# Selective scan: the rate product moved into the banks of y, y copied out in two passes, sums of a block begun later

## The chip, the cores and the metric

The kernel runs on one core of a Trainium2 chip. The metric is the device time of one execution in microseconds (us). Four compute engines work side by side, each through its own list of instructions in order: TensorE (PE: matrix products and transposes), VectorE (DVE), ScalarE (ACT) and GpSimd (POOL). Transfers are issued by these engines or by SyncE (SP) and run on 16 DMA engines. An instruction waits where a semaphore that it names has not been reached, and everything behind it on its engine waits too. PE writes its results into PSUM, a small memory in banks; 128 partitions of 1024 float32 values take two banks.

## The reference

Layer 0 is an attention over pairs, layer 1 a block with a selective scan. Nearly the whole time goes into the four scans of layer 1, cut here to what matters:

```python
delta = softplus(dts + dt_bias)                  # the "rate", one per token and channel
def step(h, inp):
    d_t, x_t, B_t, C_t = inp
    dA = exp(d_t[..., None] * As)
    h = dA * h + (d_t * x_t)[..., None] * B_t[:, :, None, :]
    y = einsum('bkdn,bkn->bkd', h, C_t)          # sum over the 16 states
    return (h, y)
# four orders of the 256 x 256 tokens: by rows, by columns, and both backwards
y = out_y[:, 0] + inv_y[:, 0] + wh_y + invwh_y
```

There are 65,536 tokens, 256 channels (two halves of 128) and 16 states. `dts` is a product of an 8-row matrix with the scan's own weights; the bias is a ninth row.

## The kernel before

`build` runs group statistics, a layer norm, the attention, a convolution, a transposition of one scratch tensor, `scans`, and `output`. `scans` (line 620) goes through the four orders one after the other, each in 64 blocks of 1024 tokens (`TB`), 256 blocks in all. A block has 32 half steps: half step `s` is state `m = s // 2` and channel half `h = s % 2`. The blocks of a scan are written out in a loop body of 18 blocks, run three times, with 4 blocks ahead of it and 6 behind; the instructions are issued in the order written (`manual_schedule`).

The work of a half step `s`, in the order of `body` (line 926):

- `recur(s)` (DVE, line 875): one scan instruction over 128 x 1024 values. It reads the decay `da` and the input `d1` and writes `hs`. After the second half DVE reduces the last column into `state`, and POOL multiplies both halves of `hs` by `cc` (the C of the reference, line 882).
- `turn(s + 1)` (PE, lines 863 and 865): fills `d1` of the next half step, 3 of its 8 pieces by a product with diagonal matrices and 5 by transposing pieces of `but`. `d1` lies in one of only two PSUM tiles `mm` (ring of two, function `mm()`), handed out in turn.
- `collect_some` (PE, line 617 in `turned`): transposes multiplied pieces of `hs` from six half steps (`LAG * NH`) earlier and adds them up in the PSUM tiles of y. Eight pieces come in for each half step; the most that are taken is 10, or what the table `share` says for this half step. The tiles of y still hold the block before until its last pieces are in (half step 5), so the pieces of a new block wait until a tile is in the set `free`.
- `decay(s + 4)` and `scale(s + 4)` (ACT, lines 856 and 852): the exponential `da` (a ring of six) and two or three of the five pieces of `but`.

The pieces of the next block's preparation are spread over these half steps by the list at the end of `begin` (line 751). Each entry is (half step, whether at its end, function). `rate(h)` (PE, line 764) is the product of the nine rows with the weights; `size(h)` (ACT, lines 773 and 774) reads it twice, into `e` (absolute value) and `delta` (positive part); `exp`, `log`, `one_plus` and `rest` are four ACT passes over 128 x 2048 values; `add` is a transfer issued by POOL (line 792) that adds `e`, `lw` or `w` to `delta` in memory; `turn_rate(i)` (PE, line 799) transposes half of the finished `delta` into an `mm` tile, and `times_x(i)` (DVE, line 803) multiplies that into `dxt`, which the next block's `scale` and `turn` read. `spread(g)` is a small ACT copy and a transfer.

In the kernel before, `rate` takes an `mm` tile, so a block hands out 36 of them: 32 for `d1`, two for the rate, two for `turn_rate`. y is four PSUM tiles of 512 values (`pys`); `evict` (ACT, line 915) copies two of them at half step 6 and two at half step 8, and puts them into `free`.

Of the kernel before, what the change touches and what calls it, by code (L numbers as in the profile page):

```python
# [35 lines left out]
P = 128  # L36
# [4 lines left out]
DI = 256  # L41
# [578 lines left out]
def scans(tc, io, c):  # L620
# [11 lines left out]
    nc = tc.nc  # L632
    TB = 1024
    NJ = TB // P
# [4 lines left out]
    PB = T // DI  # L639
    with tc.tile_pool(name="e_w", bufs=1) as wp, tc.tile_pool(name="e_1", bufs=1) as sb1, tc.tile_pool(  # L640
# [11 lines left out]
        def ring(name, n, shape, pool=wp):  # L652
            return [pool.tile(shape, F32, name=f"{name}{i}") for i in range(n)]
# [21 lines left out]
        das = ring("da", DA, [P, TB])  # L675
        hss = ring("hs", HS, [P, NH, TB])
        mms = ring("mm", 2, [P, TB], psum)
        pys = ring("y", NJ // PB, [P, PB, DI], psum)
        count = [0]

        def mm():
            count[0] += 1
            return mms[count[0] % 2]
# [67 lines left out]
        def begin(B):  # L751


            k = B.S.k
            B.pu, B.e = {}, None

            def rate(h):
                if B.e is None:  # L760
                    B.e = sb1.tile([P, NH, TB], F32, name="e")
                pu = B.pu[h] = mm()
                for q in range(0, TB, T):
                    nc.tensor.matmul(  # L764
                        pu[:, q : q + T],
                        dtw[0 : DR + 1, k, h * P : (h + 1) * P],
                        B.dt[0 : DR + 1, q : q + T],
                        start=True,
                        stop=True,
                    )  # L770

            def size(h):
                nc.scalar.activation(B.e[:, h, :], B.pu[h], AF.Abs)  # L773
                nc.scalar.activation(B.delta[:, h, :], B.pu[h], AF.Relu)

            def exp():
                nc.scalar.activation(B.e, B.e, AF.Exp, scale=-1.0)

            def log():
                B.lw = sb1.tile([P, NH, TB], F32, name="lw")  # L780
                nc.scalar.activation(B.lw, B.e, AF.Ln, bias=1.0)

            def one_plus():
                B.w = sb1.tile([P, NH, TB], F32, name="w")
                nc.scalar.activation(B.w, B.e, AF.Identity, bias=1.0)

            def rest():

                nc.scalar.activation(B.w, B.w, AF.Identity, scale=-1.0, bias=1.0)

            def add(name):
                nc.gpsimd.dma_start(out=B.delta, in_=getattr(B, name), accum_op=ALU.add)

            def turn_rate(i):
                B.pt = mm().rearrange("p (j d) -> p j d", d=DI)
                for j in range(NJ // 2):
                    for h in range(NH):
                        at = (i * NJ // 2 + j) * P
                        nc.tensor.transpose(B.pt[:, j, h * P : (h + 1) * P], B.delta[:, h, at : at + P], c.ident)

            def times_x(i):
                G = N // P
                nc.vector.tensor_tensor(  # L803
                    B.dxt[:, i * NJ // 2 : (i + 1) * NJ // 2, :].rearrange("p (w g) c -> p w g c", g=G),
                    B.pt.rearrange("p (w g) c -> p w g c", g=G),
                    B.in_order(B.xk, i, 2),
                    ALU.mult,
                )

            def spread(g):  # L810
                z = zs[0]
                first, step = B.slot(by_diagonal[0]), B.slot(by_diagonal[1]) - B.slot(by_diagonal[0])
                nc.scalar.copy(  # L813
                    z[:, P - 1 : P - 1 + GS * DJ * P].rearrange("p (m j q) -> p j m q", j=DJ, q=P)[:, :, :, 0],
                    B.bt[:, first : first + step * (DJ - 1) + 1 : step, g * GS : (g + 1) * GS],
                )
                nc.scalar.dma_start(out=B.apart(g), in_=z)

            pieces = [(4 + 6 * g, True, spread, g) for g in range(DS // GS)]
            return sorted(pieces + [  # L820
                (1, False, rate, 0),
                (1, True, size, 0),
                (3, False, rate, 1),
                (3, True, size, 1),
                (4, True, exp),
                (5, True, add, "e"),
                (9, True, log),
                (12, True, one_plus),
                (12, True, add, "lw"),
                (14, True, rest),  # L830
                (18, True, add, "w"),
                (25, False, turn_rate, 0),
                (25, True, times_x, 0),
                (27, False, turn_rate, 1),
                (27, True, times_x, 1),
            ], key=lambda x: x[:2])
# [70 lines left out]
                    collect(*x)  # L907
                    most -= 1

        def evict(B, after, part):  # L910

            n = NJ // PB // 2
            for g in range(part * n, (part + 1) * n):
                to = B.y[:, g * PB : (g + 1) * PB, :]
                nc.scalar.copy(to, pys[g])  # L915
                if after:
                    after.free.add(g)

        def add_y(B):
            nc.gpsimd.dma_start(out=B.rows(io["y"]), in_=B.as_rows(B.y), accum_op=ALU.add)  # L920

        U = NH * DS

        share = {1: 7, 3: 7, 6: 0, 7: 8, 8: 0, 25: 5, 27: 5}

        def body(blocks, before, after):

            own = len(blocks)
            at_hand = dict(enumerate(blocks + after))
            if before:  # L930
                at_hand[-1] = before
                before.free = before.started = set(range(NJ // PB))
                d1s[:] = [mms[count[0] % 2]]

            def at(u):
                x, s = divmod(u, U)
                return (at_hand[x], *divmod(s, NH)) if x in at_hand else None

            def do(f, u):
                if at(u):  # L940
                    f(*at(u))

            if before is None:
                blocks[0].load()
                blocks[0].load_tokens(0)
                blocks[0].load_tokens(1)
                blocks[0].advance(U, True)
                blocks[0].free = set(range(NJ // PB))
                blocks[1].load()
                for m in range(4):  # L950
                    fetch(blocks[0], m)
                for m in range(DG - 1):
                    diagonal(blocks[0], m)
                for u in range(2 * NH):
                    do(scale, u)
                for u in range(4):
                    do(decay, u)
                do(turn, 0)
            for x, B in enumerate(blocks):
                nxt = at_hand.get(x + 1)  # L960
                for s in range(U):
                    u = x * U + s
                    m, h = divmod(s, NH)
                    if s in (0, 8) and nxt:
                        nxt.load_tokens(s // 8)
                    if s == 21 and x + 2 in at_hand:
                        at_hand[x + 2].load()
                    if nxt:
                        nxt.advance(s, False)
                    if h == 0 and at(u + (DG - 1) * NH):  # L970
                        diagonal(*at(u + (DG - 1) * NH)[:2])
                    recur(B, m, h)
                    do(turn, u + 1)
                    if at(u - LAG * NH):
                        waiting.extend((*at(u - LAG * NH), j) for j in range(NJ))
                    collect_some(len(waiting) if s == LAG * NH - 1 else share.get(s, 10))
                    if x - 1 in at_hand and s in (6, 8):
                        evict(at_hand[x - 1], B, (s - 6) // 2)
                    if x - 1 in at_hand and s == 22:
                        add_y(at_hand[x - 1])  # L980
                    if nxt:
                        nxt.advance(s, True)
                    do(decay, u + 4)
                    if u == 0:
                        nc.scalar.preload_act_table_set("natural_log_exp_and_others")
                    do(scale, u + 2 * NH)
                    if h == NH - 1 and at(u + 1 + 3 * NH):
                        fetch(*at(u + 1 + 3 * NH)[:2])
            if not after:
                waiting.extend((*at(u), j) for u in range(own * U - LAG * NH, own * U) for j in range(NJ))  # L990
                collect_some(len(waiting))
                for part in range(2):
                    evict(blocks[-1], None, part)
                add_y(blocks[-1])
            assert not waiting


        n = NT // TB
# [160 lines left out]
```

## Time and profile before

| what | us |
|---|---|
| median of 3 runs (28149.8 to 28175.03) | 28162.98 |
| the profiled execution | 28147.05 |
| its span | 28145.4 |
| of it ahead of the scans, 0 to 4700 | 4700 |
| the scans, 4700 to 27360 | 22660 |
| the output stage, 27360 to the end | 786 |
| PE busy over the span | 25532.2 (91%) |
| DVE busy | 23715.0 (84%) |
| ACT busy | 23406.4 (83%) |
| POOL busy | 21571.6 (77%) |

The busy shares are means over stages with different limits. A PE that counts as busy need not run at full speed: matmuls are pipelined, and the column PEclk gives the clock that was granted as a share of full speed (0.976 over this span). The waits behind an engine's idle time are inferred from semaphore events, and a wait for several is put down to the one that came last. In a timeline a line is: start in us, length in us, engine, line of the kernel, operation, output and input tile, shape, how many in a row, and in square brackets the idle time ahead of it with what ended it.

### The profile page before, as it was taken

Reading aid. Unit: us, or ns where it says so; the run is one execution under the profiler, and the core shown is the slowest. Engines: PE = TensorE matmul, PEld = TensorE weight load, DVE = VectorE, ACT = ScalarE, POOL = GpSimd, SP = SyncE. Lnnn points to the kernel's source line nnn. Section 1 sums busy time; section 2 is a strip of 40 time slices with the busy share of each in tenths; the row PEclk is TensorE's granted clock in tenths of the full one; section 3 lists DMA queues with packets and bytes.
Section 4 is the critical chain, followed back from the end, with each engine's and each line's share of the span. In section 5 each row is a group of like instructions: output and inputs, shape, how many; then the busy total and the mean of one; then the engine's idle time right before and its main releaser. Section 6 shows DMA issues by size and latency. Waiting matters only on the chain. (4 is left out here: it accounts for less than half of the span.)

```text
span 28145.4 us, 510228 instructions
## 1 busy us (share of the span) xinstructions
PE 25532.2 (91%) x186250; PEld 20995.3 (75%) x186250; DVE 23715.0 (84%) x22718; ACT 23406.4 (83%) x39945; POOL 21571.6 (77%) x10118
## 2 busy tenths in 40 slices
PE   8999996999999999999999999999999999999988
PEld 3555443888888888888888888888888888888874
DVE  4777665888888888888888888888888888888887
ACT  6886223998989989989899899898998998989987
POOL 2443001998989989989899888888888888888883
PEclk9999997999999999999999999999999999999999
DMA  5112436888888888888888777777777777777775
GB/s 209 51 55 67 114 110 143 233 233 230 233 230 233 233 229 232 233 228 233 227 234 234 226 232 233 230 233 230 232 233 231 232 233 229 233 230 232 232 209 172
DMA packets 2607960, 5843.84 MB, mean 208 GB/s; under 512 B 626505, under 2 KB 1727433, under 8 KB 2475218
## 3 DMA queue, kind: packets, MB, share of 16 engines
q1 hardware_dynamic: 1682770, 3608.45, 40.5%
q0 software_dynamic: 278528, 1073.81, 19.2%
q10 hardware_dynamic: 644096, 1128.36, 11.2%
q8 instruction: 1489, 24.40, 0.3%
q14 instruction: 1077, 8.82, 0.1%
HBM read 3539.29 MB, written 1465.25 MB: 178 GB/s over the span
## 5 line engine op out<-in xcount | busy, mean ns | idle before, releaser
L882 POOL TENSOR_TENSOR hs<-hs,cc 128x1024 f32<-128x1024 f32 x8192 | 19428.7, 2460 | 2392.3 <-PE y L617 630.7
L875 DVE TENSOR_TENSOR_SCAN hs<-da,state,mm 128x1024 f32<-128x1024 f32 x8192 | 18907.3, 2338 | 2440.8 <-PE mm L865 1983.0
L856 ACT ACTIVATE da<-delta,A 128x1024 f32<-128x1024 f32 x8192 | 9348.9, 1141 | 514.2 <-ACT z L813 311.5
L852 ACT ACTIVATE but<-dxt,bt 128x256 f32<-128x256 f32 x20480 | 8961.5, 496 | 11.2 <-DVE dxt L803 10.4
L617 PE MATMUL y<-ident,hs 128*128 128x128 f32 x65536 | 8668.8, 276 | 107.7 <-POOL hs L882 31.4
L863 PE MATMUL mm<-dg,dxt 128*128 128x128 f32 x49152 | 7214.6, 284 | 979.6 <-DVE hs L875 841.5
L617 PEld LDWEIGHTS y<-ident,hs 128*128 128x128 f32 x65536 | 7493.5, 143 | 312.0 <-ACT yb L915 208.5
L863 PEld LDWEIGHTS mm<-dg,dxt 128*128 128x128 f32 x49152 | 6226.6, 194 | 1786.9 <-DVE hs L875 1429.2
L865 PE MATMUL mm<-ident,but 128*128 128x128 f32 x40960 | 6862.4, 282 | 740.2 <-ACT but L852 542.2
L865 PEld LDWEIGHTS mm<-ident,but 128*128 128x128 f32 x40960 | 4963.4, 143 | 1652.8 <-ACT but L852 1627.7
L773 ACT ACTIVATE e<-mm 128x1024 f32<-128x1024 f32 x512 | 524.2, 1024 | 1618.0 <-PE mm L764 1618.0
L385 POOL TENSOR_TENSOR an<-ex,rs 128x1024 f32<-128x1024 f32 x512 | 969.1, 1893 | 1025.2 <-PE tp L394 566.7
L500 POOL MEMSET pad<- 128x10 f32 x32 | 3.7, 116 | 1649.1 <-PE ps L537 1638.9
L764 PE MATMUL mm<-dt,dtw 9*128 9x512 f32 x2048 | 1024.6, 620 | 219.7 <-DMA bt<-mid_bk 183.9
L537 PE MATMUL ps<-pad,w 128*128 128x512 f32 x2048 | 954.9, 610 | 161.1 <-ACT xi L525 161.1
L372 ACT ACTIVATE ex<-sc,nm 128x256 f32<-128x256 f32 x2048 | 1013.7, 499 | 0.4
L355 DVE CUSTOM_DVE_ANT_0 sc<-ps,bias 128x256 f32<-128x256 f32 x2048 | 746.5, 421 | 117.2 <-PE ps L340 117.2
L394 PEld LDWEIGHTS tp<-ident,an 128*128 128x128 f32 x4096 | 467.5, 141 | 469.9 <-POOL an L385 234.7
L537 PEld LDWEIGHTS ps<-pad,w 128*128 128x128 f32 x2048 | 377.6, 194 | 580.6 <-issue 393.6
L547 DVE SCALAR_TENSOR_TENSOR acc<-xi,cw,acc 128x512 f32<-128x512 f32 x1024 | 754.7, 749 | 28.3 <-issue 1.7
L764 PEld LDWEIGHTS mm<-dt,dtw 9*128 9x128 f32 x2048 | 343.1, 186 | 577.9 <-issue 484.1
L880 DVE TENSOR_REDUCE state<-hs 128x2 f32<-128x2 f32 x4096 | 636.9, 155 | 140.3
(140 smaller groups left out, 17800.6 us busy)
## 6 DMA issues: line engine op xcount, KB each, us to landing
cc<-mid_dc SPq DMA_DIRECT2D x2048, 512.0 KB
cc<-mid_dcT SPq DMA_DIRECT2D x2048, 512.0 KB
mid_apart<-z ACTq DMA_DIRECT2D x1024, 832.0 KB
dg<-mid_apart SPq DMA_DIRECT2D x4096, 192.0 KB
xk<-mid_xk SPq DMA_DIRECT2D x512, 512.0 KB
delta<-e POOLq DMA_DIRECT2D x256, 1024.0 KB, 10.9
delta<-lw POOLq DMA_DIRECT2D x256, 1024.0 KB, 10.9
delta<-w POOLq DMA_DIRECT2D x256, 1024.0 KB, 10.5
```

The costliest lines, as they stand in the source:

```text
L372: nc.scalar.activation(exs[u][:, x, :], scs[u][:, e, jt, :], AF.Exp, scale=-1.0, bias=nms[u][:, e, jt : jt + 1], accum_out=sms[u][:, x : x ...
L385: nc.gpsimd.tensor_tensor(ans[u], exs.pop(u), bcast(rs, 2, [P, 2 * NJ, N]), ALU.mult)
L537: nc.tensor.matmul(ps.rearrange("p (r w) -> p r w", w=N), w4[:, x, h * P : (h + 1) * P], pad[:, q * rr + dy : q * rr + dy + rr, dx : dx + ...
L547: nc.vector.scalar_tensor_tensor(acc.rearrange("p (r w) -> p r w", w=N), xi[:, h, q * rr + dy : q * rr + dy + rr, dx : dx + N], cw[:, t, h ...
L617: nc.tensor.matmul(out, in_, c.ident, is_transpose=True, start=start, stop=stop, skip_group_check=True)
L764: nc.tensor.matmul(pu[:, q : q + T], dtw[0 : DR + 1, k, h * P : (h + 1) * P], B.dt[0 : DR + 1, q : q + T], start=True, stop=True,)
L852: nc.scalar.activation(bu[:, x, :], B.dxt[:, j, :], AF.Copy, scale=B.bt[:, B.slot(j), m : m + 1])
L856: nc.scalar.activation(da, B.delta[:, h, :], AF.Exp, scale=A[:, B.S.k * NH + h, m : m + 1])
L863: nc.tensor.matmul(d1[:, j * P : (j + 1) * P], B.dxt[:, j, hc], dg[:, x, :], start=True, stop=True)
L865: nc.tensor.transpose(d1[:, j * P : (j + 1) * P], bu[:, x, hc], c.ident)
L875: nc.vector.tensor_tensor_scan(o, d0, d1, state[:, m, h : h + 1], ALU.mult, ALU.add)
L882: nc.gpsimd.tensor_tensor(hs[:, x, :], hs[:, x, :], ccs[m % 4], ALU.mult)
```

## The change

The y tiles become two pairs of 1024 values each (`pairs`), in the same banks; the four old names are views of them. `rate(h)` writes into `pairs[h]` instead of an `mm` tile, after ACT has copied the previous block's y out of that pair. The copy is now one pass of 1024 values for each pair, at half steps 6 and 7. The new block's sums may use the first pair from half step 8 and the second from half step 9; `share` is set to match. The rate and all that follows from it up to the transfer of `w` moves to later half steps; `turn_rate` and `times_x` stay at 25 and 27.

```diff
-        pys = ring("y", NJ // PB, [P, PB, DI], psum)
+        pairs = ring("y", NJ // PB // 2, [P, 2 * PB, DI], psum)
+        pys = [pairs[g // 2][:, g % 2 * PB : (g % 2 + 1) * PB, :] for g in range(NJ // PB)]
...
-                pu = B.pu[h] = mm()
+                pu = B.pu[h] = pairs[h].rearrange("p j d -> p (j d)")
...
-                (1, False, rate, 0),
-                (1, True, size, 0),
-                (3, False, rate, 1),
-                (3, True, size, 1),
-                (4, True, exp),
-                (5, True, add, "e"),
-                (9, True, log),
-                (12, True, one_plus),
-                (12, True, add, "lw"),
-                (14, True, rest),
-                (18, True, add, "w"),
+                (6, True, rate, 0),
+                (7, False, size, 0),
+                (7, True, rate, 1),
+                (8, False, size, 1),
+                (8, True, exp),
+                (10, True, add, "e"),
+                (11, True, log),
+                (13, True, one_plus),
+                (15, True, rest),
+                (15, True, add, "lw"),
+                (20, True, add, "w"),
                 (25, False, turn_rate, 0),
                 (25, True, times_x, 0),
                 (27, False, turn_rate, 1),
                 (27, True, times_x, 1),
...
-        def evict(B, after, part):
-
-            n = NJ // PB // 2
-            for g in range(part * n, (part + 1) * n):
-                to = B.y[:, g * PB : (g + 1) * PB, :]
-                nc.scalar.copy(to, pys[g])
-                if after:
-                    after.free.add(g)
+        def evict(B, part):
+
+            nc.scalar.copy(B.y[:, part * NJ // 2 : (part + 1) * NJ // 2, :], pairs[part])
...
-        share = {1: 7, 3: 7, 6: 0, 7: 8, 8: 0, 25: 5, 27: 5}
+        share = {6: 0, 7: 0, 8: 8, 25: 5, 27: 5}
...
+                    if x - 1 in at_hand and s in (8, 9):
+                        n = NJ // PB // 2
+                        B.free = B.free | set(range((s - 8) * n, (s - 7) * n))
                     collect_some(len(waiting) if s == LAG * NH - 1 else share.get(s, 10))
-                    if x - 1 in at_hand and s in (6, 8):
-                        evict(at_hand[x - 1], B, (s - 6) // 2)
+                    if x - 1 in at_hand and s in (6, 7):
+                        evict(at_hand[x - 1], s - 6)
```

More of the change, by code (lines that the diff above doesn't have):

```diff
@@ L992, in body @@
                 for part in range(2):
-                    evict(blocks[-1], None, part)
+                    evict(blocks[-1], part)
                 add_y(blocks[-1])
```

## The prediction

> **What bounds the kernel now.** I read the busy time by stage first. The scans take 22660 of 28145 us, and no other stage is touched, so everything is decided there:
>
> ```profile
> 4700.00:27360.00 22660.00, 20685.80 (x161792) 18341.06 (x161792) 19988.59 (x12811) 20345.30 (x32796) 20189.41 (x9216) 0.98 0.80 231
> ```
>
> The columns after the length are PE, PE's weight loads, DVE, ACT, POOL, granted clock, DMA share and GB/s. The four engines are busy 88 to 91%: none is the bound alone, so I looked for what each waits for. The groups of instructions with their releasers, inside the scans:
>
> ```profile
> L875 DVE TENSOR_TENSOR_SCAN hs<-da,state,mm 128x1024 f32<-128x1024 f32 x8192 | 18907.3, 2338 | 2440.8 <-PE mm L865 1983.0 <-PE y L617 201.7 <-POOL hs L882 118.0
> L773 ACT ACTIVATE e<-mm 128x1024 f32<-128x1024 f32 x512 | 524.2, 1024 | 1618.0 <-PE mm L764 1618.0
> ```
>
> DVE loses 2441 us waiting for PE's `d1`; ACT loses 1618 us waiting for the rate. The timeline of DVE shows where in a block. One that begins at 15179.54:
>
> ```profile
> 15179.54 4.59 DVE L875 TENSOR_TENSOR_SCAN hs<-da,state,mm 128x1024 f32<-128x1024 f32 x2
> ...
> 15185.76 4.59 DVE L875 TENSOR_TENSOR_SCAN hs<-da,state,mm 128x1024 f32<-128x1024 f32 x2 [1.45 <-PE mm L865]
> ...
> 15192.05 4.58 DVE L875 TENSOR_TENSOR_SCAN hs<-da,state,mm 128x1024 f32<-128x1024 f32 x2 [1.51 <-PE mm L865]
> ...
> 15230.03 2.35 DVE L875 TENSOR_TENSOR_SCAN hs<-da,state,mm 128x1024 f32<-128x1024 f32 x1 [1.00 <-PE mm L865]
> ```
>
> These are scans 0, 2, 4 and 18. The first two waits are the rate's: its product sits in an `mm` tile, so `d1` of the next half step finds no tile and is made only after the scan before it. Between 8 and 18 come seven more waits (0.19 to 1.34 us, 4.4 together); there PE's own timeline waits for `but`, so ACT is late. After 18 there are only two of 0.30 us, at `times_x`. ACT is late because it was held up by the rate and then has the whole preparation to do; in this block its last wait ends here:
>
> ```profile
> 15190.57 1.02 ACT L773 ACTIVATE e<-mm 128x1024 f32<-128x1024 f32 x1 [0.61 <-PE mm L764]
> ```
>
> Scan 12 of successive blocks starts at 15039.02, 15127.14 and 15213.58, so two of three blocks take 88.1 us and one 86.4 (mean 87.5). In the long ones the granted clock drops to 0.50 for about 3.4 us after the first rate product.
>
> **Part 1: the start of a block, up to scan 18.** The rate leaves the `mm` ring, so the waits of scans 2 and 4 go. What sets scan 18 is ACT, which must finish the last `but` of state 9. The prices are ACT's start-to-start distances in the timeline: a pass of `size` 0.92, `da` 1.04, a piece of `but` 0.40, a 2048 pass 1.80, `spread` with its issue 0.62, copying a pair of y 0.94.
>
> Before, from `size(1)` at half step 3 to the `but` of half step 15: 1.84 + four copies 1.88 + four passes 7.20 + two spreads 1.24 + 13 decays 13.52 + 33 pieces 13.20 = 38.9. From 15190.57 that gives 15229.5, and 0.5 later (the last `but` to the scan, 15038.51 to 15039.02) 15230.0: the row has 15230.03. So this sum is the path.
>
> After: scans 0 to 5 run without a wait, 6 x 2.35 = 14.1; then PE does `turn(7)` (1.3) and the first rate product (1.9, from 15188.55 to 15190.46), so `size(0)` starts at 17.3. From it to half step 15: two sizes 3.68 + the second copy 0.94 + four passes 7.20 + one spread 0.62 + 9 decays 9.36 + 23 pieces 9.20 = 31.0. Scan 18 starts at 17.3 + 31.0 + 0.5 = 48.8. Before it is 50.5 in the short block and 52.2 in a long one (15003.32 to 15055.48), mean 51.6. **Gain 2.8 us a block.** The single 1024 copy has no row; two 512 copies take 0.94 and a 1024 pass from PSUM 0.92, so I take 0.94 and no gain.
>
> New waits on PE: the rate products wait for the copies of y, and behind the second stands `turn(9)`. ACT reaches that copy after `size(0)`, at 20.1; the product is done at 22.0 and scan 9 starts some 2.4 us late. ACT hides this: with it DVE would be at scan 18 at 18 x 2.35 + 2.4 = 44.7, four ahead of ACT. Without that cover it costs 2.4 x 256 = 614 us.
>
> The second product has a smaller cover. Between copy and `size(1)` ACT has one decay and three pieces, 2.2 us, against 2.0 of product and latency. At half clock a product is up to twice as long (longest record 1217 ns against 588), and ACT, the path here, waits up to 1.6. The clock has fallen after less idle time than PE has here, but mostly after the product. Between 0 and 1.6 I take 0.3.
>
> The sums: 24 pieces wait at half step 8, 14 after half step 9, as before. Their order is the same, so `hs` is freed in time. SP issues the same transfers in the same places.
>
> **Part 2: the end of the preparation.** POOL issues the three adds two, two and one state later: `e` after the multiplications of half step 9 instead of 5, `lw` after 15 instead of 11, `w` after 19 instead of 17. `turn_rate` stays where it is and reads the sum. The rows of before:
>
> ```profile
> 15059.34 0.87 POOL L792 DMA_DIRECT2D delta<-w  x1
> 15060.49 9.41 POOL L882 TENSOR_TENSOR hs<-hs,cc 128x1024 f32<-128x1024 f32 x4 [0.28 <-DVE state L880]
> ...
> 15071.98 1.09 PE L799 MATMUL mm<-ident,delta 128*128 128x128 f32 x8
> ```
>
> ```profile
> delta<-w POOLq DMA_DIRECT2D x256, 1024.0 KB, 10.5
> ```
>
> The add of `w` takes 10.5 us to land: 15069.8, two before PE reads it at 15071.98. After the change it stands behind two of the four multiplications: 15060.49 + 4.7 = 15065.1, landing at 15075.6. PE, in order, waits 3.6 us at its first transpose. `times_x` starts at 15076.7 instead of 15074.27, and `turn(26)` behind it lets scan 26 start at 15078.15 instead of 15075.80: 2.35 us lost at full clock. Nothing hides it: `dxt` and `d1` both stand behind this wait.
>
> It will not be full clock. Where PE idled 4.09 us at a loop's end it came back like this:
>
> ```profile
> 15626.26 1.65 PE L863 MATMUL mm<-dg,dxt 128*128 128x128 f32 x6 [4.09 <-DVE hs L875]
> 15627.70 1.27 PE L865 MATMUL mm<-ident,but 128*128 128x128 f32 x5
> ```
>
> against 0.94 and 0.71 elsewhere, and stayed at half clock for 3.5 us. The eight transposes then take 1.8 instead of 0.9, and most of `turn(26)` runs at half: scan 26 at 15079.9. **Loss 4.1 us a block.**
>
> The wait of `w` for `lw` is shorter too: four half steps, 9.4 us and 0.55 of issue, plus two waits of about 1.0 that DVE still has before 18 and 16, make 12 us against 10.9 of landing. Free; without those waits `w` is 0.9 later still.
>
> The Trainium skill, "TensorE: Matmul & The Clock Gate", section "Part 1: The HAM clock gate", says that the clock halves after at least one idle window of about 3.4 us, and that the windows run freely. By that rule a wait of 3.6 us would seldom hold a whole window, the loss would be 2.35, and the sum a gain of about 0.15 us a block. The rows speak against it: after the rate product the clock fell with 0.26 us of idle time.
>
> **The sum.** -2.8 + 0.3 + 4.1 = +1.6 us a block, 256 blocks: +410 us on a span of 28145, 28555. The median of the runs stands 18 above that span: about **28570**. Its own range is 28350 to 28850.
>
> **The rivals.** (1) *The add of `w` is hidden after all.* Price: at its least landing time, 7.5 us (a quiet moment at a scan's start), PE waits 0.6, loses little, and 2.8 a block remains: 27450. At full clock alone it is -2.8 + 2.35 = -0.45: 28050. It decides from a landing of 9.0 us at half clock. For it: the clock was never seen under just this wait. Against: the three adds land in 10.5 to 10.9 at three different places of the block. 25%. (2) *Gain and loss cancel*, for a landing near 9: 28160. 8%. (3) *More is late*: the second product at half clock in every block (+1.3 over my 0.3) and `w` slowed by the add of y that POOL now issues 4.7 us after it, up to the longest landing of 12.7 (+2.2): at most 29470, half of it 29000. For it: DMA is busy 80% in the scans. Against: one queue serves adds in order. 13%. My forecast has 54%.
>
> **Chances and range.** A measurement of this kernel tells 0.2% (56 us) from no change. Slower 0.67 (forecast and the third), same 0.07, faster 0.26. The range reaches into the first rival and half into the third: 27850 to 29000.
>
> **What would show it.** Right: DVE has no wait at scans 2 and 4, one of over 2 us at scan 9, waits again at 14 to 18, and a new one at `times_x` ended by PE's line 800, with PE there waiting for the transfer of `w` and a granted clock of 0.5 behind it; scan 18 comes 49 us after scan 0. Wrong: PE does not wait for `w`, or the clock stays at 1.0 (then the time is near 28050), or scan 18 comes later than 51 (ACT waits at `size(1)`).

## The result, and the profile after

The changed kernel takes 29565.53 us (median of 4 runs, 29547.44 to 29580.84), the kernel before 28164.25 (four runs here, one more than in the table above): a ratio of 1.0498 with a 95% interval of 1.0479 to 1.0516. It is slower, as forecast, but by 1401 us instead of 410: 5.5 us a block instead of 1.6. The profiled execution has a span of 29573.5 us.

The busy time of the scans, with the columns as before (the loop code is a few lines shorter, so most line numbers are one lower or higher):

```profile
4700.00:28780.00 24080.00, 21219.38 (x161777) 19240.37 (x161778) 19933.13 (x12811) 20540.29 (x32282) 20214.46 (x9215) 0.92 0.75 217
```

DVE, ACT and POOL do the same work as before to within 1%, in 1420 us more. The granted clock falls from 0.98 to 0.92. The groups of the profile's page, busy time, mean, idle time and its releaser:

```profile
L876 DVE TENSOR_TENSOR_SCAN hs<-da,state,mm 128x1024 f32<-128x1024 f32 x8192 | 18870.9, 2337 | 2380.2 <-PE mm L866 2105.8
...
L800 PE MATMUL mm<-ident,delta 128*128 128x128 f32 x4096 | 762.5, 348 | 1710.2 <-DMA delta<-w 1710.2
...
L804 DVE TENSOR_TENSOR dxt<-mm,xk 128x1024 f32<-128x1024 f32 x512 | 625.5, 1222 | 1588.7 <-PE mm L800 1587.9
...
L774 ACT ACTIVATE e<-y 128x1024 f32<-128x1024 f32 x512 | 524.6, 1025 | 358.8 <-PE y L765 358.0
```

ACT's wait for the rate has gone from 1618 to 359 us, so the change does what it says. In its place PE waits 1710 us for the transfer of `w`, 6.7 a block, and DVE 1588 us behind it at `times_x`, where it had waited 45. The same two groups of the kernel before:

```profile
L799 PE MATMUL mm<-ident,delta 128*128 128x128 f32 x4096 | 546.8, 277 | 66.7 <-DMA delta<-w 37.3 <-DVE hs L875 2.8
...
L803 DVE TENSOR_TENSOR dxt<-mm,xk 128x1024 f32<-128x1024 f32 x512 | 625.8, 1222 | 44.9 <-PE mm L799 44.1 <-issue 0.8
```

DVE's waits ahead of the scans are as long as before in sum, but lie elsewhere. DVE's timeline of one block (scans 0, 9, 18, 24 and 25, then `times_x` and scan 26):

```profile
15045.84 4.58 DVE L876 TENSOR_TENSOR_SCAN hs<-da,state,mm 128x1024 f32<-128x1024 f32 x2
...
15071.95 2.35 DVE L876 TENSOR_TENSOR_SCAN hs<-da,state,mm 128x1024 f32<-128x1024 f32 x1 [4.34 <-PE mm L866]
...
15095.75 4.58 DVE L876 TENSOR_TENSOR_SCAN hs<-da,state,mm 128x1024 f32<-128x1024 f32 x2 [1.01 <-PE mm L866]
...
15109.85 4.59 DVE L876 TENSOR_TENSOR_SCAN hs<-da,state,mm 128x1024 f32<-128x1024 f32 x2
...
15121.31 1.23 DVE L804 TENSOR_TENSOR dxt<-mm,xk 128x1024 f32<-128x1024 f32 x1 [6.69 <-PE mm L800]
15123.73 2.35 DVE L876 TENSOR_TENSOR_SCAN hs<-da,state,mm 128x1024 f32<-128x1024 f32 x1 [1.19 <-PE mm L866]
```

Scan 18 comes 49.9 us after scan 0 in this block, 50.3 in the mean of all blocks (51.6 before, forecast 49.1 with the 0.3). Then the block loses everything: between the end of scan 25 (15114.44) and scan 26 lie 9.3 us here and 8.5 in the mean, where the kernel before has 1.6. That is a mean loss of 6.8, where the forecast had 4.1. POOL's timeline of this block shows how `w` came to be so late:

```profile
15094.31 0.87 POOL L793 DMA_DIRECT2D delta<-lw  x1
15094.99 4.93 POOL L883 TENSOR_TENSOR hs<-hs,cc 128x1024 f32<-128x1024 f32 x2
15100.75 4.73 POOL L883 TENSOR_TENSOR hs<-hs,cc 128x1024 f32<-128x1024 f32 x2 [0.83 <-DVE state L881]
15106.53 0.87 POOL L793 DMA_DIRECT2D delta<-w  x1 [1.05 <-DMA delta<-lw]
```

POOL is through with the multiplications at 15105.5 and then waits 1.05 us for `lw`, which takes 12.2 us to land; `w` itself takes 12.8. Over all blocks POOL waits 1.8 us there, and `w` takes 11.35 in the mean (median 11.5). PE's timeline of the same block:

```profile
15119.34 1.94 PE L800 MATMUL mm<-ident,delta 128*128 128x128 f32 x8 [7.19 <-DMA delta<-w]
15121.07 1.49 PE L864 MATMUL mm<-dg,dxt 128*128 128x128 f32 x6
15122.35 1.27 PE L866 MATMUL mm<-ident,but 128*128 128x128 f32 x5
```

The 1.94 us for eight transposes (1.09 before) are the half clock: the granted clock is 0.50 in the windows from 15115.53 to 15120.53.

### The profile page after: what moved, and what is told of

Same layout as the page of the kernel before. It is cut to its first block, busy times and chain, and to the rows that moved or that the text cites. A ratio compares the mean times of both kernels' runs of the same rounds, so it can differ in the third digit from the quotient of the medians.

```text
span 29573.5 us, 508968 instructions
## 1 busy us (share of the span) xinstructions
PE 26074.8 (88%) x186250; PEld 21898.8 (74%) x186250; DVE 23656.5 (80%) x22718; ACT 23604.1 (80%) x39433; POOL 21601.9 (73%) x10118
## 5 line engine op out<-in xcount | busy, mean ns | idle before, releaser
L864 PE MATMUL mm<-dg,dxt 128*128 128x128 f32 x49152 | 7630.0, 294 | 458.3 <-DVE hs L876 239.4
L864 PEld LDWEIGHTS mm<-dg,dxt 128*128 128x128 f32 x49152 | 6573.6, 203 | 1510.6 <-DVE hs L876 693.0
L617 PEld LDWEIGHTS y<-ident,hs 128*128 128x128 f32 x65536 | 7665.2, 145 | 3.3 <-POOL hs L883 3.3
L866 PE MATMUL mm<-ident,but 128*128 128x128 f32 x40960 | 6553.8, 285 | 272.1 <-ACT but L853 175.8
L800 PE MATMUL mm<-ident,delta 128*128 128x128 f32 x4096 | 762.5, 348 | 1710.2 <-DMA delta<-w 1710.2
L800 PEld LDWEIGHTS mm<-ident,delta 128*128 128x128 f32 x4096 | 633.7, 182 | 1765.1 <-issue 1764.6
L804 DVE TENSOR_TENSOR dxt<-mm,xk 128x1024 f32<-128x1024 f32 x512 | 625.5, 1222 | 1588.7 <-PE mm L800 1587.9
L765 PE MATMUL y<-dt,dtw 9*128 9x512 f32 x2048 | 1307.2, 768 | 560.7 <-ACT yb L913 374.8
L765 PEld LDWEIGHTS y<-dt,dtw 9*128 9x128 f32 x2048 | 403.7, 217 | 1003.1 <-issue 528.6
L774 ACT ACTIVATE e<-y 128x1024 f32<-128x1024 f32 x512 | 524.6, 1025 | 358.8 <-PE y L765 358.0
## 6 DMA issues: line engine op xcount, KB each, us to landing
delta<-lw POOLq DMA_DIRECT2D x256, 1024.0 KB, 12.2
delta<-w POOLq DMA_DIRECT2D x256, 1024.0 KB, 11.5
```

The source lines that it names most:

```text
L617: nc.tensor.matmul(out, in_, c.ident, is_transpose=True, start=start, stop=stop, skip_group_check=True)
L765: nc.tensor.matmul(pu[:, q : q + T], dtw[0 : DR + 1, k, h * P : (h + 1) * P], B.dt[0 : DR + 1, q : q + T], start=True, stop=True,)
L864: nc.tensor.matmul(d1[:, j * P : (j + 1) * P], B.dxt[:, j, hc], dg[:, x, :], start=True, stop=True)
L866: nc.tensor.transpose(d1[:, j * P : (j + 1) * P], bu[:, x, hc], c.ident)
```

## The experiments

All times are medians beside runs of the kernel before on the same chip. That kernel took between 28154.75 and 28164.25 in the four groups of runs, so times from different groups can be set against each other to some 10 us. The theory after the result was that nearly all of the loss is the chain of three adds (called A); the rival, that it sits at the start of the block (B). The first four kernels were to tell these apart and to price the parts of the chain.

**e1: the adds earlier.**

```diff
-                (10, True, add, "e"),
+                (8, True, add, "e"),
...
-                (15, True, add, "lw"),
+                (12, True, add, "lw"),
-                (20, True, add, "w"),
+                (18, True, add, "w"),
```

> The changed kernel with the three adds to delta issued earlier: e at half step 8, lw at 12, w at 18, each as soon as its ACT pass is done and at a whole transfer's distance. Everything else of the change stays. Theory A (the loss is the late chain of three adds: PE's transposes of delta wait 6.7 us a block for w, and run at half clock behind it): w is issued at about scan 17's end + 5 us, lands before scan 24 ends, the 1710 us of PE waiting for w fall under 300, and the time falls to 27600 to 27900, under the kernel before. Theory B (the loss sits at the start of the block: scan 9 waits 4.3 us behind the second rate product, at half clock): the time stays above 28700.

27815.97 us against 28156.45: 0.9877 (0.9861 to 0.9894). The changed kernel with an earlier chain is 1750 us faster than the changed kernel, and 340 us faster than the kernel before. PE's group of transposes of `delta` in e1:

```profile
L800 PE MATMUL mm<-ident,delta 128*128 128x128 f32 x4096 | 546.8, 277 | 66.0 <-DMA delta<-w 36.5 <-DVE hs L876 2.8
```

The 1710 us of waiting for `w` are 37, and the mean of a transpose is 277 ns again, not 348. A stands, and B falls: scan 9 still waits, 4.69 us in a block of e1, and the kernel is faster all the same.

```profile
15167.22 2.35 DVE L876 TENSOR_TENSOR_SCAN hs<-da,state,mm 128x1024 f32<-128x1024 f32 x1 [4.69 <-PE mm L866]
```

It also splits the result: the start of the block gains 340 / 256 = 1.3 us a block, and the late chain costs 1750 / 256 = 6.8. The traces say the same: from scan 0 to scan 18 e1 takes 50.3 us in the mean, as the changed kernel does, against 51.6 before, and between scans 25 and 26 it takes 1.6, as the kernel before.

**e2: PE kept at work while it waits for w.**

```diff
                 B.pt = mm().rearrange("p (j d) -> p j d", d=DI)
+                for r in range(0 if i else 56):
+                    nc.tensor.transpose(B.pt[:, r % 4, r // 4 % 2 * P : (r // 4 % 2 + 1) * P], c.ident, c.ident)
```

> The changed kernel with 56 transposes of the identity ahead of the first transposes of delta, into the same PSUM tile, which the real ones then overwrite: PE works about 6.1 us in the time in which it waits for w. Only the clock behind the wait is changed. Theory A with the clock as I priced it (1.8 us a block): no half clock behind the wait, time 29050 to 29150. If the wait for the transfer alone is the loss and the half clock is hidden: unchanged within 80 us of the changed kernel. If the transposes themselves are late: slower.

29139.37 us, 1.0354 (1.0337 to 1.0371): 426 us below the changed kernel, 1.7 a block. The real transposes in e2:

```profile
L802 PE MATMUL mm<-ident,delta 128*128 128x128 f32 x4096 | 542.7, 276 | 105.4 <-DMA delta<-w 103.5
```

They take 276 ns, full clock, and DVE's wait at `times_x` goes from 1588 to 1398 us (the rest of the gain is in `turn(26)`). Work that computes nothing makes the kernel faster, because it holds the clock (0.955 over the run instead of 0.923); `w` lands in 11.5 us as before. The forecast had priced the half clock at 4.1 - 2.35 = 1.75.

**e3: the late chain in the kernel before.** The rate stays in the `mm` tiles at half steps 1 and 3.

```diff
-                (4, True, exp),
-                (5, True, add, "e"),
-                (9, True, log),
-                (12, True, one_plus),
-                (12, True, add, "lw"),
-                (14, True, rest),
-                (18, True, add, "w"),
+                (8, True, exp),
+                (10, True, add, "e"),
+                (11, True, log),
+                (13, True, one_plus),
+                (15, True, add, "lw"),
+                (15, True, rest),
+                (20, True, add, "w"),
```

> The kernel before with only the later half steps of the passes and the adds (exp 8, e 10, log 11, one_plus 13, rest and lw 15, w 20); the rate stays in the mm ring at half steps 1 and 3, y in four tiles. Theory A: all of the late wait comes without any of the gain at the start of the block, some 7 us a block over the kernel before: 29700 to 30200, slower than the changed kernel. Theory B: within 150 us of the kernel before.

29544.74 us, 1.0495 (1.0478 to 1.0513). A again, but with a miss of 155 us below the expected range: it is as slow as the changed kernel, not slower. PE waits less for `w` here than after the change:

```profile
L799 PE MATMUL mm<-ident,delta 128*128 128x128 f32 x4096 | 750.5, 345 | 1439.6 <-DMA delta<-w 1439.5
```

These are 1440 us instead of 1710. In its timeline POOL waits 0.2 to 0.3 us ahead of the add of `w` where the changed kernel waits 1.05, since DVE, slower between `lw` and `w`, gives the add of `lw` more time, and `lw` lands in 11.5 us instead of 12.2. So the price of a late chain depends on what runs beside it: 5.4 us a block here (5.6 at the end of the block, with 0.3 won back ahead of scan 18), 6.8 there.

**e4: the add of y at half step 28.**

```diff
-                    if x - 1 in at_hand and s == 22:
+                    if x - 1 in at_hand and s == 28:
                         add_y(at_hand[x - 1])
```

> The changed kernel with the add of y issued at half step 28 instead of 22, so that it no longer runs beside the add of w. If y's 1 MB slows w: w lands in about 10.5 us instead of 11.5 to 12.8, and the time falls by 250 to 600 us. If one queue serves them in order, as the prediction argued: unchanged within 80 us.

29542.51 us, 1.0492 (1.0474 to 1.0509): 23 us below the changed kernel, and the two intervals overlap. The add of `w` lands in 11.2 us instead of 11.5. The transfer that POOL issues 5 us after it, on the same queue, costs it 0.3 us at most.

**e6: lw one pair of multiplications earlier.**

```diff
-                (15, True, add, "lw"),
+                (14, True, add, "lw"),
```

> The changed kernel with the add of lw at half step 14 instead of 15, one pair of multiplications earlier for POOL; w stays at 20. If w's wait for lw is part of the loss (POOL waits some 1.8 us a block ahead of the add of w, which the prediction called free): POOL no longer waits there, w lands 1 to 1.8 us earlier, time 29100 to 29310. If it is free: within 80 us of the changed kernel, 29565.

29201.99 us, 1.0370 (1.0354 to 1.0386): 364 us below the changed kernel, 1.4 a block. POOL's timeline:

```profile
15099.03 0.87 POOL L793 DMA_DIRECT2D delta<-lw  x1 [0.34 <-issue]
15099.64 9.65 POOL L883 TENSOR_TENSOR hs<-hs,cc 128x1024 f32<-128x1024 f32 x4
15109.75 4.72 POOL L883 TENSOR_TENSOR hs<-hs,cc 128x1024 f32<-128x1024 f32 x2 [0.46 <-DVE state L881]
15114.39 0.90 POOL L793 DMA_DIRECT2D delta<-w  x1
```

The add of `w` follows the multiplications without a wait. Issuing `lw` earlier, and so ending the wait that the prediction called free, is worth 1.4 us a block.

**e8: another transfer moved away from w.** In the changed kernel `spread(3)` issues its 832 KB at 15108.24, 1.7 us after the add of `w` (1.3 as a median of all blocks). In the kernel before it came 8.6 us after it. ACT's timelines, of the changed kernel and of the kernel before, and the landing in the changed kernel:

```profile
15108.24 0.33 ACTq L818 DMA_DIRECT2D mid_apart<-z  x1
...
15067.97 0.33 ACTq L817 DMA_DIRECT2D mid_apart<-z  x1
...
delta<-w POOLq DMA_DIRECT2D x256, 1024.0 KB, 11.5
```

```diff
-            pieces = [(4 + 6 * g, True, spread, g) for g in range(DS // GS)]
+            pieces = [((4, 10, 16, 28)[g], True, spread, g) for g in range(DS // GS)]
```

> The changed kernel with the last of the four small ACT copies and its transfer (832 KB, spread(3)) at half step 28 instead of 22, so that it no longer runs while the add of w is under way; in the kernel before it started 8.6 us after w, at w's landing. If this transfer slows w: w lands in about 10.5 us instead of 11.5, PE waits a good 1 us less, time 29250 to 29350. If it does not: within 80 us of the changed kernel, 29565, and what lengthens the landing stays open.

28994.11 us, 1.0302 (1.0285 to 1.0319): 571 us below the changed kernel, twice what was expected. The transfers of e8 (KB each, median us from issue to landing):

```profile
delta<-w POOLq DMA_DIRECT2D x256, 1024.0 KB, 9.0
```

The add lands in 9.0 us instead of 11.5, less than the 10.5 of the kernel before. PE's wait for it falls from 1710 to 1166 us, nearly all of the 571. The transfer on ACT's queue costs it 2.5 us; y on its own queue costs 0.3.

**e5: both copies of y together, on top of e1.** This one is for the start of the block, which gained 1.3 us where 2.5 were forecast. In the changed kernel PE's two rate products stand like this:

```profile
15061.38 1.98 PE L765 MATMUL y<-dt,dtw 9*128 9x512 f32 x4
15063.29 0.94 PE L864 MATMUL mm<-dg,dxt 128*128 128x128 f32 x6
15064.06 0.71 PE L866 MATMUL mm<-ident,but 128*128 128x128 f32 x5
15066.29 2.88 PE L765 MATMUL y<-dt,dtw 9*128 9x512 f32 x4 [1.52 <-ACT yb L913]
15069.10 1.65 PE L864 MATMUL mm<-dg,dxt 128*128 128x128 f32 x6
```

PE waits 1.52 us for the second copy, and in the second product the clock falls (2.88 instead of 1.98, then 1.65 instead of 0.94).

```diff
-                    if x - 1 in at_hand and s in (6, 7):
-                        evict(at_hand[x - 1], s - 6)
+                    if x - 1 in at_hand and s == 6:
+                        evict(at_hand[x - 1], 0)
+                        evict(at_hand[x - 1], 1)
```

> The kernel of e1 with both copies of y at half step 6, one after the other, so that PE need not wait 1.5 us for the second copy between the two rate products. If the missing 1.1 us of the block's start (scan 18 at 49.9 to 50.7 us after scan 0 instead of the 49.1 that the prediction had) is ACT's wait of 0.7 to 1.6 us at the second size, behind a second rate product that starts late and runs at half clock: that wait goes, scan 18 comes at about 49.1, and the time falls by 200 to 320 us to 27500 to 27620. It tests the cover too: scan 9's wait of about 5 us should shrink to under 1, that is by 1000 us and more in sum, and if ACT hides it, as the prediction says, the time moves by no more than the 300 above. If scan 9's wait counts, the time falls by 800 or more.

27471.25 us, 0.9755 (0.9742 to 0.9768): the fastest kernel of this study, 345 us below e1 (25 more than the most that was expected) and 689 below the kernel before. In its timelines the second product follows without a wait at full clock (PE), and scan 18 comes 48.65 us after scan 0 (DVE):

```profile
15078.81 0.94 PE L864 MATMUL mm<-dg,dxt 128*128 128x128 f32 x6
15079.58 0.71 PE L866 MATMUL mm<-ident,but 128*128 128x128 f32 x5
15080.22 1.98 PE L765 MATMUL y<-dt,dtw 9*128 9x512 f32 x4
```

```profile
15061.44 4.58 DVE L876 TENSOR_TENSOR_SCAN hs<-da,state,mm 128x1024 f32<-128x1024 f32 x2
...
15083.75 2.35 DVE L876 TENSOR_TENSOR_SCAN hs<-da,state,mm 128x1024 f32<-128x1024 f32 x1 [0.97 <-ACT but L853]
...
15110.09 2.35 DVE L876 TENSOR_TENSOR_SCAN hs<-da,state,mm 128x1024 f32<-128x1024 f32 x1 [1.00 <-PE mm L866]
```

ACT's wait at `size` falls from 375 us in e1 to 66, and that is the gain: 345 us against 309. Scan 9's wait falls from 4.69 to 0.97 us in these blocks and by 828 us in the sum over the run, and that does not show in the time beyond the 345. So ACT did hide it. One block in five (52 of 255) still waits some 4 us there; in as many the second product runs at half clock.

**e7: e1 with the copies in halves.**

```diff
-            nc.scalar.copy(B.y[:, part * NJ // 2 : (part + 1) * NJ // 2, :], pairs[part])
+            for g in range(part * NJ // PB // 2, (part + 1) * NJ // PB // 2):
+                nc.scalar.copy(B.y[:, g * PB : (g + 1) * PB, :], pys[g])
```

> The kernel of e1 with each copy of 1024 values made as two of 512, in the same places; so it undoes the single pass alone. The prediction took no gain from the single pass (0.94 us either way): within 40 us of e1, 27816. If a whole pass saves a start-up of ACT, this is slower by up to 0.1 us a copy, 50 us.

27824.19 us, 0.9880 (0.9865 to 0.9895), 8 us above e1 with overlapping intervals. The two whole passes alone are worth nothing that can be measured.

## Why the prediction was wrong in size

**The start of the block** was forecast at -2.8 + 0.3 and measured at -1.3 (e1). The sum over ACT's work is right: where nothing disturbs it, in e5, scan 18 comes at 48.65 us for 48.8 forecast, and e5 gains 689 / 256 = 2.7 a block for 2.8. The term that was mis-sized is the second rate product at half clock, 0.3 taken from between 0 and 1.6. What e5 takes away, the half clock together with the wait of 1.5 us that goes before it, is 345 / 256 = 1.3, near the upper end. The reason given, that the clock would fall mostly after the product, was wrong: in 216 of 256 blocks of the changed kernel it falls within it.

**The cover for scan 9** was right (e1, e5): a wait of 4 to 5 us, longer than the 2.4 forecast, that costs nothing.

**The end of the preparation** was forecast at 4.1 and measured at 6.8 (the changed kernel less e1). The mechanism was right: PE stands in order before the transposes of `delta` and waits for `w`, and then runs at half clock (e2: 1.7 us a block, forecast 1.75). What failed is the time of the landing, in two steps:

- "Free", of the wait of `w` for `lw`. I compared 12 us of distance with 10.9 of landing. POOL was ready 11.2 us after the issue in the block shown, and `lw` took 12.2. Over all blocks POOL waited 1.8 us. e6 got 1.4 a block back: the wait is gone there, but `w` lands 0.4 later (11.73 instead of 11.35 in the mean).
- The landing time of 10.5, taken over from before. Moving the add moves it under other transfers: 11.5 as a median, 12.8 in the block shown. (The 15065.1 to which the prediction adds it is 15065.2 by its own terms; nothing hangs on that.) The prediction looked for such a transfer only on POOL's queue (the third rival, the add of y), and that one costs 0.3 us of landing at most (e4). The one that counts is ACT's `spread(3)`, which stayed where it was while `w` moved next to it (e8: 2.5 us of landing, 571 us of time).

With these two terms put right the forecast's own sum comes out, in the changed kernel and in four of the experiments. The table has means over all blocks of each trace, in us; the sum is 4.1, plus POOL's wait ahead of the add of `w`, plus what the landing of `w` exceeds 10.5 by; the last column is the time between the end of scan 25 and scan 26, less the 1.64 of the kernel before.

| kernel | wait for `lw` | landing of `w` | sum | measured |
|---|---|---|---|---|
| changed | 1.77 | 11.35 | 6.72 | 6.82 |
| e3 | 0.53 | 11.54 | 5.67 | 5.64 |
| e4 | 1.66 | 11.24 | 6.50 | 6.59 |
| e6 | 0.00 | 11.73 | 5.33 | 5.43 |
| e8 | 1.81 | 9.18 | 4.59 | 4.57 |

**The clock.** The rule in "TensorE: Matmul & The Clock Gate", section "Part 1: The HAM clock gate", of the Trainium skill was set against the rows for a wait of 3.6 us. In the changed kernel that wait came out at 6.7 us on average, longer than its window, and the clock fell, as both say. The shorter waits of e8 tell the two apart: of its 56 blocks in which PE waited 3.4 to 4.0 us, 35 had half clock through all eight transposes behind the wait and 17 had full clock. By the rule a whole window would seldom fit into such a wait, so the forecast was nearer, though its half clock does not come in every block. At the rate products the rows stand against the rule too: the clock fell with an idle time of 1.52 us and two products of nine rows within 8 us. What makes it fall there is not shown.

**The rivals.** The third, more is late, held 13% and is the nearest: its first half (the second product) happened in five blocks of six, and its second did with another transfer than the one named. Its half-way price of 29000 set the upper end of the range, and the time lies above that and above its full price of 29470. The first rival's price of 27450 leaves out the 0.3 of the second product; with it the sum is 27520. e1, where `w` is in time, took 27816.

## What to carry to other kernels

When a step is moved later, follow it to the last instruction that reads its result, and recompute each landing among the transfers that will then run beside it, on all queues, those of engines that the change doesn't touch too: a landing time read from a profile belongs to its place. In a chain of adds into the same bytes each is issued after the one before has landed, so a short gap between two issues becomes a wait of the issuing engine and makes the next landing later. Here the move of the product was worth 2.4% once its tail was issued early and its two copies stood together; the form in which it came cost 5%.

## What the runs showed of the hardware

- The same 1 MB add of `w` took 9.0 (e8), 10.5 (before) and 11.5 us (changed) to land, as medians, and single adds of the three took from 6.9 to 14.9. 832 KB issued 1.3 us later (median) on ACT's queue cost it 2.5 us, 1 MB issued 5 us later on its own queue 0.3.
- Transposes that fill a wait made the kernel faster by 426 us, with the landing of `w` unchanged at 11.5 us: 276 ns for each real transpose behind them instead of 348.
- The clock fell to half without a long idle stretch: 1.52 us of waiting, or less, between two rate products of nine rows was enough in 216 of 256 blocks of the changed kernel, and with no wait between them 203 of 256 blocks of e5 kept full clock in the second product.
- Behind waits of 3.4 to 4.0 us (e8) the clock was half in 35 of 56 blocks and full in 17; behind waits of over 5 us it was always half (e8, 38 blocks).
